# Two product groups to a PSUM bank, longer leads, and an accumulator that one engine touches: a graph network on one Trainium2 core

## The chip, the core and the metric

The kernel runs on one core of one Trainium2 chip. A core has five engines with a queue of instructions each: TensorE (PE in the profile, with its weight loads as PEld), VectorE (DVE), ScalarE (ACT), GpSimd (POOL) and SyncE (SP). PSUM, where TensorE writes its products, has eight banks of 512 float32 columns in 128 partitions. The metric is the device time of one execution in microseconds; lower is better. Three runs of the kernel before took 34,501.49, 34,504.76 and 34,556.67 us.

## The reference

There are 30,000 nodes with 128 features and 960,000 edges that are sorted by destination. Two layers are computed: a relational convolution, applied twice, and a gated one. Cut to what matters:

```python
def rel(h, basis, coeff, bias):              # basis [8,128,128], coeff [32,8]
    W = einsum('rb,bdf->rdf', coeff, basis)  # one matrix for each of 32 edge types
    msg = einsum('nd,rdf->nrf', h, W)[src, etype32] * weight
    return segment_sum(msg, dst) + bias

h = relu(layernorm(x))
x = x + rel(relu(rel(h, basis1, coeff1, bias1)), basis2, coeff2, bias2)

h = relu(layernorm(x))
for t in range(4):                           # one set of matrices for each of 4 edge types
    k, q, v = h @ Wk[t] + bk[t], h @ Wq[t] + bq[t], h @ Wv[t] + bv[t]
    msg = where(etype4 == t, sigmoid(k[dst] + q[src]) * v[src], 0)
    outs[t] = segment_sum(msg, dst) + h @ Ws[t] + b[t]
x = x + mean(outs)
```

## The kernel before

Edges are taken in tiles of 128, three tiles to a **group** (384 edges) and five groups to a **block**. Because edges are sorted, the destinations of a group lie within a window of 32 nodes. A preparation computes each edge's place in its window (`reld`) and index columns. Then come three **passes** over all edges: `c1` and `c2` (the two relational convolutions, `rel_body`) and `g` (the gated one, `gate_body`). Each pass is a loop of 25 iterations of 20 blocks, so 500 blocks, 2,500 groups and 7,500 tiles in all. An iteration is cut into four stages of five blocks.

The rows of the edges' sources are fetched from HBM by POOL, one indirect DMA for each tile (`gather`, L114), into a group's buffer `hg` (passes one and two) or `qv` (pass three, 1 KB a row); there are ten such buffers. The running sums of all nodes stand in SBUF as `agg` (128 features x 31,440 nodes). `add_windows` (L361) adds a block's five windows of 32 columns to it, at offsets that registers hold.

*Passes one and two.* With a group's rows come the edges' eight basis coefficients: `types` (L380) loads a block's edge types, `onehot` (L387, L392) makes a one-hot on VectorE and multiplies it with `coeff` on TensorE into `pc`, and `coefficients` (L401) scales them to `ce`. For each tile VectorE builds `sb` (L441), which holds the coefficient where the window column equals the edge's place, else zero, and TensorE multiplies it with the tile's rows into `pa` (L447; 8 x 32 columns, three tiles added up). ScalarE copies `pa` into the block's `ab` (L451). Once a block, `bases_out` (L409) multiplies `ab` with the eight basis matrices into `po`.

*Pass three.* For each group SP loads the window's keys `kw` (L485). `onehot` (L488, L494) compares the block's codes `kb` with `ic` and places with `iw`; `keys` (L501) multiplies one-hot and `kw` on TensorE into `pk`; VectorE adds the gathered queries (L542); ScalarE takes the sigmoid (L543). `sums` (L510, L512) multiplies by the values on VectorE and adds up by window on TensorE into `po`.

The order of all this is written out by hand (`tc.manual_schedule`); each engine runs its instructions in that order, and the framework adds the semaphore waits. The constants `iw` and `ic` stand in a PSUM tile `cp`, which also holds `pc`. `pa` has three banks, `po` two, `pk` four.

Beside the groups, `steps` finishes nodes whose sums are complete, 120 at a time: `after_first` writes the hidden layer and restarts the sums, `after_second` makes layer norm and the tables of keys, queries and values, `after_third` writes the result. Each such chain is spread over the following groups by the numbers in its list, and a new one starts every `PERIOD` (9) groups.

Of the kernel before, what the change touches and what calls it, by code (L numbers as in the profile page):

```python
# [9 lines left out]
F32 = mybir.dt.float32  # L10
# [36 lines left out]
PERIOD = NG * VB // NPI - 1  # L47
# [22 lines left out]
def kernel(  # L70
# [177 lines left out]
    def node_weights(nodew):  # L248

        wall = nodew.tile([P, 3, T, D], F32, name="wall")  # L250
        ball = nodew.tile([P, 3, T, D], F32, name="ball")
        for a, (w, b) in enumerate(((wk, bk), (wq, bq), (wv, bv))):
            nc.sync.dma_start(wall[:, a], w.rearrange("t d f -> d t f"))
            nc.scalar.dma_start(ball[:, a].rearrange("p t f -> p (t f)"), rows_of(b, P))
        nc.vector.tensor_add(ball[:, 0], ball[:, 0], ball[:, 1])
        for w in (wall, ball):
            nc.vector.tensor_scalar(w[:, 2], w[:, 2], 1.0 / T, None, op0=ALU.mult)
        four = nodew.tile([P, T, D], F32, name="four")
        nc.sync.dma_start(four, ws.rearrange("t d f -> d t f"))
        wsm = nodew.tile([P, D], F32, name="wsm")  # L260
        nc.vector.tensor_reduce(wsm, four.rearrange("p t f -> p f t"), AX.X, ALU.add)
        nc.vector.tensor_scalar(wsm, wsm, 1.0 / T, None, op0=ALU.mult)
        return wall, ball, wsm

    def node_tables(pool, ps, wall, ball, hn, krows, qvrows):
# [8 lines left out]
        for a in range(3):  # L274
            pw = ps.tile([P, T, D], F32, name="pw", bufs=4)
            nc.tensor.matmul(pw.rearrange("p t f -> p (t f)"), lhsT=hT,
                             rhs=wall[:, a].rearrange("p t f -> p (t f)"), start=True, stop=True)
            if a == 1:
                nc.scalar.copy(to[a], pw)
            else:  # L280
                nc.vector.tensor_add(to[a], pw, ball[:, a])
# [8 lines left out]
    def sorted_path():  # L290
        with ExitStack() as all_:
# [8 lines left out]
            def edge_pass(name, body, after, banks):  # L300


                with ExitStack() as held:
                    weights = held.enter_context(tc.tile_pool(name=f"{name}_w", bufs=1))
                    steps, run = after(weights), body(weights)
                    with tc.tile_pool(name=f"{name}_io", bufs=NQ) as io, \
# [8 lines left out]
                        nc.vector.tensor_copy(ic, icol)  # L315
                        with tc.For_i(0, NI, 1, iteration_sync="staggered") as i:
                            with tc.manual_schedule():
# [5 lines left out]
                                assert W < TQ * 4 * B and max(todo) < NG  # L323
# [5 lines left out]
                                run(i, io, pool, ps, cp, iw, ic, beside)  # L329
# [33 lines left out]
            def rel_body(table, weights, cof):  # L363
                def start(npool):
                    bas = npool.tile([P, B, D], F32, name="bas")
                    nc.scalar.dma_start(bas, weights.rearrange("b d f -> d b f"))
                    return lambda *args: body(bas, *args)

                def body(bas, i, io, pool, ps, cp, iw, ic, beside):
# [8 lines left out]
                    def types(s):  # L378
                        er[s] = pool.tile([P, TQ, TP], I32, name="er")
# [5 lines left out]
                    def onehot(s):  # L385
                        oh[s] = pool.tile([P, TQ, TP], F32, name="oh")
                        nc.vector.tensor_scalar(oh[s], er[s], icol4, None, op0=ALU.is_equal)  # L387
                        at = (1 + s % 2) * TQ * 4 * B
                        pc[s] = cp[:TP, at:at + TQ * 4 * B].rearrange("p (c q b) -> p c q b",
                                                                      c=TQ, q=4)  # L390
# [15 lines left out]
                    def bases_out(s):  # L406
                        po[s] = ps.tile([P, S, W], F32, name="po")
# [7 lines left out]
                    types(0)  # L415
                    onehot(0)
                    coefficients(0)
                    types(1)
                    onehot(1)
                    for s in range(NS):  # L420
# [9 lines left out]
                        if s + 2 < NS:  # L430
                            types(s + 2)
                        ab[s] = pool.tile([P, B, S, W], F32, name="ab")
                        for g in range(S):
# [4 lines left out]
                            pa = ps.tile([P, B, W], F32, name="pa", bufs=3)  # L438
                            for j in range(G):
                                sb = pool.tile([TP, B, W], F32, name="sb", bufs=12)  # L440
# [15 lines left out]
                            if g == 3 and s + 2 < NS:  # L456
                                onehot(s + 2)
                            if g == 3 and s > 1:
                                add_windows(po[s - 2], base[(s - 2) // SB], s - 2)
# [4 lines left out]
                    for s in (NS - 2, NS - 1):  # L464
# [3 lines left out]
            def gate_body(i, io, pool, ps, cp, iw, ic, beside):  # L468
# [7 lines left out]
                def types(s):  # L476
                    kb[s] = pool.tile([P, S, GE + GAP], F32, name="kb")[:, :, :GE]
# [20 lines left out]
                def keys(n):  # L498
                    pk[n] = ps.tile([TP, G, D], F32, name="pk", bufs=4)
# [5 lines left out]
                def sums(n):  # L505
                    s, g = n // S, n % S
                    if g == 0:
                        po[s] = ps.tile([P, S, W], F32, name="po")
# [9 lines left out]
                for n in range(S):  # L518
                    window(n)
                onehot(0)  # L520
                keys(0)
                for n in range(NG):
# [8 lines left out]
                    if g == 0 and s + 1 < NS:  # L531
                        types(s + 1)
# [7 lines left out]
                    if n + 1 < NG:  # L540
                        keys(n + 1)
# [4 lines left out]
                    if g == 1 and s + 1 < NS:  # L546
                        onehot(s + 1)
                    if g == 4 and s:
                        add_windows(po[s - 1], base[(s - 1) // SB], s - 1)
# [5 lines left out]
                add_windows(po[NS - 1], base[NQ - 1], NS - 1)  # L555


            def after_first(weights):

                def steps(at, pool, ps):  # L560
                    xt = pool.tile([VB, D], F32, name="xt", bufs=2)
                    r = pool.tile([P, VB], F32, name="r")
                    h = pool.tile([VB, D], F32, name="h")
                    cols, rows = agg[:, ds(at, VB)], ds(at, VB)
# [5 lines left out]
                    def relu():  # L570
                        nc.scalar.activation(r, cols, AF.Relu, bias=b1c)
# [7 lines left out]
                    def copy():  # L579
                        nc.scalar.copy(h, got["pr"])  # L580
                        nc.vector.tensor_scalar(cols, got["px"], b2c, None, op0=ALU.add)
# [4 lines left out]
                    return (0, load), (1, relu), (3, turn), (4, copy), (5, store)  # L586
                return steps

            def after_second(weights):
# [9 lines left out]
                def steps(at, pool, ps):  # L599
                    cols, rows = agg[:, ds(at, VB)], ds(at, VB)  # L600
                    xs = pool.tile([P, VB], F32, name="xs", bufs=2)
# [4 lines left out]
                    hT = pool.tile([P, VB], F32, name="hT")  # L606
                    kt = pool.tile([VB, T, D + GAP], F32, name="kt")[:, :, :D]
                    qvt = pool.tile([VB, T, 2 * D + GAP], F32, name="qvt")[:, :, :2 * D]
                    got = {}
# [5 lines left out]
                    def copy():  # L615
                        nc.scalar.copy(xs, cols)

                    def rows_():
                        nc.tensor.transpose(bank("px", VB, D), xs, ident)

                    def stats():
                        nc.vector.bn_stats(st, got["px"])
                        nc.vector.bn_aggr(mv, st)
                        nc.scalar.activation(rs, mv[:, 1:2], AF.Sqrt, bias=eps[:VB])

                    def norm_():
                        nc.vector.reciprocal(rs, rs)
                        nc.vector.tensor_scalar(hn, got["px"], mv[:, 0:1], rs, op0=ALU.subtract,
                                                op1=ALU.mult)

                    def turn():
                        nc.tensor.transpose(bank("pt", P, VB), hn, ident[:VB, :VB])

                    def relu():
                        nc.scalar.activation(hT, got["pt"], AF.Relu)

                    def weight(a):
                        def go():
                            nc.tensor.matmul(bank(a, VB, T * D), lhsT=hT,  # L639
                                             rhs=wall[:, a].rearrange("p t f -> p (t f)"),  # L640
                                             start=True, stop=True)
                        return go

                    def biased(a, to):
                        def go():
                            pw = got[a].rearrange("p (t f) -> p t f", t=T)
                            if a == 1:
# [285 lines left out]
```

## Time and profile before

| | |
|---|---|
| median of three runs | 34,504.76 us |
| the profiled execution's own time | 34,720.42 us |
| its span | 34,718.6 us |
| mean granted TensorE clock | 0.673 of full speed |
| busy: TensorE / weight loads / VectorE / ScalarE / POOL | 20,388 / 17,659 / 12,654 / 3,605 / 21,314 us |
| gathers for `hg` (L114) | 15,000, 14,224 us busy, 948 ns each |
| gathers for `qv` (L114) | 7,500, 7,088 us busy, 945 ns each |
| `sb` on VectorE (L441) | 15,000, 475 ns each |
| product matmuls (L447) | 30,000 instructions, 466 ns each |
| copies of products on ScalarE (L451) | 5,000, 373 ns each |

All durations come from this one profiled execution, whose own time is 216 us above the median of the runs. Lines of a timeline give start and duration in us, engine, line, operation, output and inputs, how many were merged, and in brackets how long the engine had been idle and what released it. A line of the list of waits gives who waited for whom: total us, times, longest. A "TensorE" matmul in float32 appears as two instructions.

### The profile page before, as it was taken

The page shows a single profiled execution, that of the slowest core. Times are in us where ns is not written, and L with a number is a line of the kernel's source. Part 1 is how long each engine was busy: PE and PEld are TensorE (multiplying, and loading weights), DVE is VectorE, ACT ScalarE, POOL GpSimd, SP SyncE. Part 2 cuts the span into 40 slices and gives each one's busy share as a digit, 9 for nine tenths or more (in the row PEclk, how much of TensorE's full clock was granted, in tenths as well). Part 3 has the DMA queues.
Part 4 walks back from the last instruction along what each step waited for, and adds up shares of the span by engine and source line. Part 5 has one row for each costly group of instructions (what it writes and reads, how often), then busy time and mean ns, then how long its engine had stood idle before and what let it go on. Part 6 is the DMA issues. An engine that isn't in the chain of part 4 may idle for free. (4 is left out here: it accounts for less than half of the span.)

```text
span 34718.6 us, 320544 instructions
## 1 busy us (share of the span) xinstructions
PE 20388.3 (59%) x87408; PEld 17658.9 (51%) x87408; DVE 12654.0 (36%) x33403; ACT 3604.7 (10%) x9717; POOL 21313.7 (61%) x22513
## 2 busy tenths in 40 slices
PE   3555555555555566666666666665555555555555
PEld 2444444444444445545445555545555555555555
DVE  4333333333333333333333333333333333333333
ACT  1000000000000011111111111111111111111111
POOL 3666666666666566666666666656666666666665
PEclk8777777777777777777777777765555555555555
DMA  3222222222222222222222222234444444444444
GB/s 111 60 60 60 59 61 60 60 59 60 59 60 59 68 73 73 73 73 73 73 73 72 73 73 73 73 103 144 143 144 144 145 144 145 144 144 143 143 143 140
DMA packets 2168060, 3244.36 MB, mean 93 GB/s; under 512 B 550283, under 2 KB 1540859, under 8 KB 2166350
## 3 DMA queue, kind: packets, MB, share of 16 engines
q0 software_dynamic: 840000, 1967.52, 21.2%
q1 hardware_dynamic: 982940, 997.80, 8.8%
q10 hardware_dynamic: 343410, 258.04, 2.6%
q8 instruction: 853, 13.98, 0.2%
q14 instruction: 857, 7.02, 0.1%
HBM read 2969.29 MB, written 252.28 MB: 93 GB/s over the span
## 5 line engine op out<-in xcount | busy, mean ns | idle before, releaser
L114 POOL DMA_INDIRECT hg<-h,idx x15000 | 14224.3, 948 | 8721.2 <-issue 4498.6
L447 PE MATMUL pa<-sb,hg 128*128 128x256 f32 x30000 | 9229.5, 466 | 5599.4 <-issue 2652.1
L447 PEld LDWEIGHTS pa<-sb,hg 128*128 128x128 f32 x30000 | 6930.6, 240 | 7333.1 <-issue 2969.4
L114 POOL DMA_INDIRECT qv<-qvtab,qi x7500 | 7087.9, 945 | 4645.7 <-issue 2252.6
L441 DVE SCALAR_TENSOR_TENSOR sb<-cp,relc,ce 128x256 f32<-128x256 f32 x15000 | 6124.2, 475 | 6625.4 <-remote 4458.6
L512 PE MATMUL po<-sel,msg 128*128 128x32 f32 x15000 | 3460.4, 387 | 4649.2 <-DVE msg L510 3763.7
L512 PEld LDWEIGHTS po<-sel,msg 128*128 128x128 f32 x15000 | 3424.0, 328 | 4936.1 <-DVE msg L510 3937.4
L501 PE MATMUL pk<-kw,kb 128*128 128x128 f32 x15000 | 3969.9, 438 | 241.1 <-DVE kb L488 183.3
L542 DVE TENSOR_TENSOR pk<-pk,qv 128x384 f32<-128x384 f32 x2500 | 1404.8, 562 | 7008.3 <-remote 4711.3
L451 ACT COPY ab<-pa 128x256 f32<-128x256 f32 x5000 | 1818.4, 373 | 20240.9 <-remote 9335.6
L501 PEld LDWEIGHTS pk<-kw,kb 128*128 128x128 f32 x15000 | 3464.0, 331 | 243.8 <-issue 243.8
L409 PE MATMUL po<-ab,bas 128*128 128x160 f32 x16000 | 2425.9, 306 | 456.7 <-ACT ab L451 243.9
L409 PEld LDWEIGHTS po<-ab,bas 128*128 128x128 f32 x16000 | 2356.3, 196 | 542.9 <-ACT ab L451 264.9
L361 DVE TENSOR_TENSOR agg<-agg,po 128x32 f32 x7500 | 1398.1, 186 | 2853.5 <-remote 789.9
L392 PE MATMUL cp<-coeff,oh 128*128 128x32 f32 x8000 | 1314.0, 294 | 1786.3 <-issue 1299.6
L392 PEld LDWEIGHTS cp<-coeff,oh 128*128 128x128 f32 x8000 | 1387.6, 235 | 1813.7 <-issue 1610.4
L543 ACT ACTIVATE pk<-pk 128x384 f32<-128x384 f32 x2500 | 1185.3, 475 | 9401.4 <-DVE pk L542 5999.8
L639 PE MATMUL bank<-wall,hT 128*120 128x512 f32 x1572 | 1011.8, 764 | 729.5 <-issue 286.6
L510 DVE TENSOR_TENSOR msg<-pk,qv 128x384 f32<-128x384 f32 x2500 | 1364.5, 546 | 137.7 <-remote 130.1
L488 DVE TENSOR_TENSOR kb<-kb,cp 128x1920 f32<-128x1920 f32 x500 | 1071.5, 2143 | 50.2 <-issue 30.4
L639 PEld LDWEIGHTS bank<-wall,hT 128*120 128x120 f32 x1572 | 347.2, 235 | 1008.1 <-issue 543.2
L650 DVE TENSOR_TENSOR kt<-bank,ball 120x512 f32<-120x512 f32 x262 | 181.1, 691 | 1457.7 <-remote 497.6
(77 smaller groups left out, 3740.7 us busy)
## 6 DMA issues: line engine op xcount, KB each, us to landing
kb<-kcode SPq DMA_DIRECT2D x500, 960.0 KB
er<-in_et_row SPq DMA_DIRECT2D x1000, 256.0 KB
hg<-h,idx POOLq DMA_INDIRECT x15000
kw<-ktab SPq DMA_DIRECT2D x2500, 64.0 KB
qvtab<-qvt ACTq DMA_DIRECT2D x262, 480.0 KB
qv<-qvtab,qi POOLq DMA_INDIRECT x7500
ktab<-kt ACTq DMA_DIRECT2D x262, 240.0 KB
xt<-in_x SPq DMA_DIRECT2D x262, 60.0 KB
```

The source lines that it names most:

```text
L114: nc.gpsimd.indirect_dma_start(out=to, out_offset=None, in_=table, in_offset=bass.IndirectOffsetOnAxis(ap=idx, axis=0))
L361: nc.vector.tensor_add(to, to, po[:, g, :])
L392: nc.tensor.matmul(pc[s][:, c].rearrange("p q b -> p (q b)"), lhsT=oh[s][:, c, :], rhs=cof.rearrange("p q b -> p (q b)"), start=True, stop ...
L409: nc.tensor.matmul(po[s].rearrange("p s w -> p (s w)"), lhsT=bas[:, b, :], rhs=ab[s][:, b].rearrange("p s w -> p (s w)"), start=(b == 0), ...
L441: nc.vector.scalar_tensor_tensor(sb, iw[:TP].unsqueeze(1).to_broadcast([TP, B, W]), relc[:, t0 + j:t0 + j + 1], ce[s].rearrange("p q c b - ...
L447: nc.tensor.matmul(pa.rearrange("p b w -> p (b w)"), lhsT=hg[:, j, :], rhs=sb.rearrange("p b w -> p (b w)"), start=(j == 0), stop=(j == G ...
L451: nc.scalar.copy(ab[s][:, :, g, :], pa)
L501: nc.tensor.matmul(pk[n][:, j, :], lhsT=kb[n // S][:, n % S, j * TP:(j + 1) * TP], rhs=kw[n], start=True, stop=True)
L510: nc.vector.tensor_mul(msg, pk[n], qv[n][:, :, 1, :])
L512: nc.tensor.matmul(po[s][:, g, :], lhsT=msg[:, j, :], rhs=sel[s][:, g * G + j, :], start=(j == 0), stop=(j == G - 1))
L542: nc.vector.tensor_add(pk[n], pk[n], qv[n][:, :, 0, :])
L639: nc.tensor.matmul(bank(a, VB, T * D), lhsT=hT, rhs=wall[:, a].rearrange("p t f -> p (t f)"), start=True, stop=True)
```

## The change

- **Product groups.** `pa` was a tile with three buffers of one bank each. It becomes eight halves of four fixed one-bank tiles, `pa0` to `pa3`; group number n of an iteration takes half n mod 8.
- **Sums.** In passes one and two `po` was a tile with two banks; it becomes three thirds of one bank, `pb`. In pass three `po` becomes two parts of the tile `cp`, and the two banks go to `pk`, which has six instead of four.
- **Leads.** In passes one and two edge types and one-hot run three blocks ahead instead of two (`er` and `oh` with three buffers, `sb` with sixteen instead of twelve), and the windows of a block are added three blocks later instead of two. In pass three keys are multiplied three groups ahead instead of one, `kb` has three buffers, the one-hot moves from a block's group 1 to group 0, and the windows of a block are added at group 0 two blocks later instead of at group 4 one block later.
- **Node steps.** `agg` is read and written by VectorE alone; copies on either side bring the values to and from the other engines. The chain of `after_second` is spread over 28 groups instead of 11, with its products leaving PSUM by ScalarE and its biases added by VectorE in SBUF. `PERIOD` is 8. The loading of the weights uses a temporary pool.

The diff, cut to its core:

```diff
-PERIOD = NG * VB // NPI - 1
+PERIOD = 8
...
                 def start(npool):
                     bas = npool.tile([P, B, D], F32, name="bas")
...
+                    def fixed(cp, cps):
+                        n = TQ * 4 * B
+                        pc = [cp[:TP, q * n:(q + 1) * n].rearrange("p (c q b) -> p c q b",
+                                                                   c=TQ, q=4) for q in (1, 2)]
+                        n = B * W
+                        pa = [cps.tile([P, 2 * n], F32, name=f"pa{q}") for q in range(4)]
+                        pa = [t[:, q * n:(q + 1) * n].rearrange("p (b w) -> p b w", b=B)
+                              for t in pa for q in range(2)]
+                        n = S * W
+                        pb = cps.tile([P, 4 * D], F32, name="pb")
+                        po = [pb[:, q * n:(q + 1) * n].rearrange("p (s w) -> p s w", s=S)
+                              for q in range(3)]
+                        return lambda *args: body(bas, pc, pa, po, *args)
+                    return fixed
...
-                        er[s] = pool.tile([P, TQ, TP], I32, name="er")
+                        er[s] = pool.tile([P, TQ, TP], I32, name="er", bufs=3)
...
-                        oh[s] = pool.tile([P, TQ, TP], F32, name="oh")
+                        oh[s] = pool.tile([P, TQ, TP], F32, name="oh", bufs=3)
...
-                        po[s] = ps.tile([P, S, W], F32, name="po")
+                        po[s] = pos[s % 3]
...
-                            pa = ps.tile([P, B, W], F32, name="pa", bufs=3)
+                            pa = pas[(s * S + g) % 8]
                             for j in range(G):
-                                sb = pool.tile([TP, B, W], F32, name="sb", bufs=12)
+                                sb = pool.tile([TP, B, W], F32, name="sb", bufs=16)
...
-                            if g == 3 and s + 2 < NS:
-                                onehot(s + 2)
-                            if g == 3 and s > 1:
-                                add_windows(po[s - 2], base[(s - 2) // SB], s - 2)
+                            if g == 3 and s + 3 < NS:
+                                onehot(s + 3)
+                            if g == 3 and s > 2:
+                                add_windows(po[s - 3], base[(s - 3) // SB], s - 3)
...
+            def gate_start(cp, cps):
+                n = S * W
+                po = [cp[:, 2 * W + q * n:2 * W + (q + 1) * n].rearrange("p (s w) -> p s w", s=S)
+                      for q in range(2)]
+                return lambda *args: gate_body(po, *args)
...
-                    kb[s] = pool.tile([P, S, GE + GAP], F32, name="kb")[:, :, :GE]
+                    kb[s] = pool.tile([P, S, GE + GAP], F32, name="kb", bufs=3)[:, :, :GE]
...
-                    pk[n] = ps.tile([TP, G, D], F32, name="pk", bufs=4)
+                    pk[n] = ps.tile([TP, G, D], F32, name="pk", bufs=6)
...
-                        po[s] = ps.tile([P, S, W], F32, name="po")
+                        po[s] = pos[s % 2]
...
-                    if n + 1 < NG:
-                        keys(n + 1)
+                    if n + 3 < NG:
+                        keys(n + 3)
                     nc.vector.tensor_add(pk[n], pk[n], qv[n][:, :, 0, :])
                     nc.scalar.activation(pk[n], pk[n], AF.Sigmoid)
                     if n > 1:
                         sums(n - 2)
-                    if g == 1 and s + 1 < NS:
+                    if g == 0 and s + 1 < NS:
                         onehot(s + 1)
-                    if g == 4 and s:
-                        add_windows(po[s - 1], base[(s - 1) // SB], s - 1)
+                    if g == 0 and s > 1:
+                        add_windows(po[s - 2], base[(s - 2) // SB], s - 2)
...
     # after_first
-                        nc.scalar.activation(r, cols, AF.Relu, bias=b1c)
+                        nc.vector.tensor_scalar(r, cols, b1c, 0.0, op0=ALU.add, op1=ALU.max)
...
-                        nc.vector.tensor_scalar(cols, got["px"], b2c, None, op0=ALU.add)
+                        nc.scalar.activation(fresh, got["px"], AF.Identity, bias=b2c)
...
+                    def restart():
+                        nc.vector.tensor_copy(cols, fresh)
...
-                    return (0, load), (1, relu), (3, turn), (4, copy), (5, store)
+                    return (0, load), (1, relu), (3, turn), (4, copy), (5, store), (9, restart)
...
     # after_second
-                    return ((1, copy), (2, rows_), (3, stats), (4, norm_), (5, turn), (6, relu),
-                            (7, weight(0)), (7, weight(1)),
-                            (8, biased(0, kt)), (8, biased(1, qvt[:, :, :D])),
-                            (8, weight(2)), (8, part),
-                            (9, biased(2, qvt[:, :, D:])), (9, own), (9, store(knode, kt)),
-                            (10, store(qvnode, qvt)))
+                    return (
+                        (0, lambda: nc.vector.tensor_copy(xs, cols)),
+                        (1, lambda: nc.tensor.transpose(bank("px", VB, D), xs, ident)),
+                        (2, lambda: nc.scalar.copy(xr, got["px"])),
+                        (6, stats),
+                        (7, lambda: nc.scalar.activation(rs, mv[:, 1:2], AF.Sqrt, bias=eps[:VB])),
+                        (11, norm_),
+                        (12, lambda: nc.tensor.transpose(bank("pt", P, VB), hn,
+                                                         ident[:VB, :VB])),
+                        (13, lambda: nc.scalar.activation(hT, got["pt"], AF.Relu)),
+                        (18, lambda: weight(0)),
+                        (19, lambda: nc.scalar.copy(kt, types(0))),
+                        (21, lambda: weight(1)),
+                        (22, lambda: nc.scalar.copy(qvt[:, :, :D], types(1))),
+                        (22, lambda: weight(2)),
+                        (23, lambda: nc.vector.tensor_add(kt, kt, ball[:VB, 0])),
+                        (23, lambda: nc.scalar.copy(vt, types(2))),
+                        (24, lambda: store(knode, kt)),
+                        (24, lambda: nc.tensor.matmul(bank("po", P, VB), lhsT=wsm, rhs=hT,
+                                                      start=True, stop=True)),
+                        (25, lambda: nc.scalar.activation(part, got["po"], AF.Identity, bias=bsc)),
+                        (26, lambda: nc.vector.tensor_add(vt, vt, ball[:VB, 1])),
+                        (27, lambda: store(qvnode, qvt)),
+                        (27, lambda: nc.vector.tensor_add(cols, xs, part)))
...
     # after_third
-                        nc.scalar.copy(c, agg[:, ds(at, VB)])
+                        nc.vector.tensor_copy(c, agg[:, ds(at, VB)])
```

## The prediction, made before the changed kernel was run

> **What bounds the kernel now.** I first cut the span at the first and last gather of each pass (busy time by window: every engine, then TensorE's clock, DMA share, GB/s).
>
> ```profile
> 335.00:11576.00 11241.00, 6348.05 (x27428) 5469.35 (x27429) 3800.81 (x11223) 1010.60 (x2992) 7127.53 (x7500) 0.73 0.23 60
> 11630.00:22948.00 11318.00, 7191.12 (x29420) 5680.44 (x29421) 4378.82 (x12715) 1179.33 (x3490) 7096.52 (x7500) 0.78 0.27 73
> 23080.00:34682.00 11602.00, 6720.55 (x30168) 6431.34 (x30168) 4199.89 (x8471) 1326.13 (x3019) 7087.92 (x7500) 0.51 0.47 144
> ```
>
> Each pass issues 7500 gathers from POOL. One is busy 0.95 us and in an undisturbed stream the next starts 0.30 us later, so a block of 15 gathers needs 18.75 us. The passes take 22.5, 22.6 and 23.2 us a block (11,241, 11,318 and 11,602 over 500). POOL thus stands still 3.7, 3.9 and 4.45 us a block, 6.0 ms in all: no change of waits can win more. Then the list of all waits:
>
> ```profile
> ACT ab L451 <- remote: 9335.6, 1058, 70.1
> ...
> POOL hg L114 <- issue: 4498.6, 12552, 332.7
> DVE sb L441 <- remote: 4458.6, 491, 32.9
> ...
> POOL hg L114 <- remote: 2025.0, 828, 5.7
> POOL qv L114 <- DVE msg L510: 1752.4, 448, 15.6
> ...
> DVE sb L441 <- PE cp L392: 1631.9, 335, 18.2
> ```
>
> "Remote" is a semaphore update that matches no recorded end of work, and it holds ScalarE for 9.3 ms. The timeline of one block of pass one shows whose it is:
>
> ```profile
> 6007.55 1.46 PE L447 MATMUL pa<-sb,hg 128*128 128x256 f32 x6
> 6009.06 1.47 PE L447 MATMUL pa<-sb,hg 128*128 128x256 f32 x6
> 6010.36 0.97 PE L392 MATMUL cp<-coeff,oh 128*128 128x32 f32 x8
> 6016.74 0.94 POOL L114 DMA_INDIRECT hg<-h,idx  x1 [0.30 <-issue]
> 6020.76 0.65 ACT L451 COPY ab<-pa 128x256 f32<-128x256 f32 x2 [14.81 <-remote]
> 6020.82 0.34 DVE L581 TENSOR_SCALAR agg<-bank,b2c 128x120 f32 x1 [14.39 <-remote]
> 6020.99 0.95 POOL L114 DMA_INDIRECT hg<-h,idx  x1 [3.31 <-remote]
> 6021.12 4.79 DVE L441 SCALAR_TENSOR_TENSOR sb<-cp,relc,ce 128x256 f32<-128x256 f32 x12
> ```
>
> TensorE's products of groups 2 and 3 are recorded as done at 6009.0 and 6010.5, yet ScalarE's two copies, VectorE and POOL all wait until 6020.8. TensorE's completions become visible ten microseconds late, and then together, about 3 us after POOL's stream of gathers stopped (at 6017.7) for want of a free `hg`. One block later it repeats. The cycle is: POOL uses up its ten buffers and stops, the late completions arrive, buffers come free, POOL restarts. Why completions lag while gathers stream the profile doesn't tell; that each block holds about one such stop it does (idle POOL over 1 us: 604, 741 and 607 times in the passes of 500 blocks). Pass three:
>
> ```profile
> 28019.03 1.63 PE L501 MATMUL pk<-kw,kb 128*128 128x128 f32 x6
> 28024.51 0.95 POOL L114 DMA_INDIRECT qv<-qvtab,qi  x1 [0.31 <-issue]
> 28028.15 0.57 DVE L542 TENSOR_TENSOR pk<-pk,qv 128x384 f32<-128x384 f32 x1 [9.49 <-remote]
> 28028.63 0.55 DVE L510 TENSOR_TENSOR msg<-pk,qv 128x384 f32<-128x384 f32 x1
> 28029.44 0.95 POOL L114 DMA_INDIRECT qv<-qvtab,qi  x1 [3.99 <-DVE msg L510]
> 28030.02 2.14 DVE L488 TENSOR_TENSOR kb<-kb,cp 128x1920 f32<-128x1920 f32 x1
> ```
>
> Here VectorE's add waits for late keys until 2.7 us after POOL stopped at 28025.5; add and `msg` then free a `qv` within 1.3 us. The one-hot (L488) comes after that release, in the shadow of the running gathers.
>
> **The change part by part.** *Sums in `cp` (pass three).* `po` moves into the tile from which L488 and L494 read `ic` and `iw`. That columns of one tile don't overlap doesn't help: L441 reads only `iw` and L392 writes only `pc`, both in `cp`, yet the last wait above stands between them, and no `sb` of group 4 in the 900 blocks that have one starts before that L392 ends. So the one-hot and add_windows, now at group 0 right behind sums(n-2), wait for the sums just issued, the newest work in TensorE's queue. Behind the one-hot on VectorE are the five adds into `agg`, the next add and the next `msg`, which frees the `qv` that POOL wants. When this wait falls into the late state, the chain from the completions to POOL grows by L488 2.14 + L494 0.65 + five adds 5 x 0.19, 3.7 us, less what add and `msg` overlap. New stop: 2.7 + 3.7 + 1.1 + 0.2 = 7.7 us, less the ordinary 0.30: 7.4 against 4.45 a block, +2.95 us, 500 times: **+1.5 ms**. Least: 0 if the wait ends while POOL has buffers; most +1.85 ms (3.7 x 500).
>
> *Keys three groups ahead, six `pk`, three `kb`.* The add's wait (4.7 ms on remote, 1.6 ms on L501) disappears there, but the one-hot inherits it: keys(n+3) stands ahead of sums(n-2) on TensorE. Gain 0 as long as that wait is once a block; if it weren't, at most 4.45 - 3.2, 0.6 ms. On SP's queue the loads keep their places: `kw` for group n+5 is issued at group n, so keys(n+3) have two groups of lead (7.5 us) instead of four, and the third `kb` lets the 960 KB load of codes go a block earlier. TensorE waited 20 us for `kw` in the whole pass; I take 0, and if `kw` came late it would add to the same stop.
>
> *Two product groups in a bank.* By the same evidence L447 of every odd group waits for ScalarE's copy of the even one, 0.37 us plus two hand-overs; behind it on TensorE queue bases_out and the next coefficients. 2500 pairs x 0.37 = 0.9 ms of TensorE's time, which its 56 to 64% busy share hides while completions are prompt. In the late state it stops TensorE from running ahead, so fewer products are finished when POOL stops. From none to one more stop of 3.0 us in every second block (1000 blocks: +1.5 ms).
>
> The Trainium skill speaks against this part: "Perfetto Trace Analysis", Optimizing Tensor Performance, asks independent groups to rotate through different PSUM banks so that one's evacuation overlaps the next one's matmuls. By that rule all 0.9 ms would be paid. The copy row sits in before beside other products, three banks apart, so no run here shows that yet.
>
> *`po` in `pb`, coefficients three blocks ahead.* add_windows at group 3 now waits for the bases_out of the same block's group 1; VectorE would wait at group 4 for L392 anyhow, so five adds (0.95 us) move behind the late completions. POOL is released there by TensorE, not by VectorE: 0 to 0.9 ms, taken 0.1. The third `er`, `oh` and 16 `sb` buy nothing, because the group 4 wait on `cp` stays.
>
> *Node steps spread out, `agg` left to VectorE.* This removes L581's wait (1128 us remote in pass one), the waits of the adds on ScalarE (562 us on `xs`) and of L650 on fresh products. What can be won is the stops beyond one a block: 104 x 3.0 + 241 x 2.5 = 0.9 ms. I take 0.6, since the L392 wait remains. The added copies (0.3 to 0.7 us, 262 times) lie on ScalarE, busy 10%, and VectorE, 36%. Weight loading changes once, nothing.
>
> I take +0.9 for the pairs, between its ends because pass two, with its chain of node matmuls, already has 137 stops more than pass one and loses only 0.1 ms by them. Sum: 34.72 + 1.5 + 0.9 + 0.1 - 0.6 = 36.6 ms for a profiled execution (34,720 now). The median of the runs is 0.6% below it, 34,505: **36,400 us**.
>
> **The rivals.** *Faster.* If the one-hot's wait ends while POOL still has buffers, since keys are issued three groups earlier and VectorE runs ahead, passes one and two win 0.9 and pass three 0.6: 33,000. Deciding point: the completions that sums(n-2) needs must come within 18 us without a stop. For it: long waits on keys exist today. Against: completions came only after a stop in the blocks shown.
>
> *Much slower.* Pairs cost a second stop in every block of passes one and two: 1000 x 3.0 = 3.0 ms, with pass three 39,000. For it: TensorE is blocked at every second group. Against: pass two above.
>
> *No effect.* Stops are set by POOL's ten buffers alone, which stay: 34,500.
>
> **How the numbers follow.** Forecast 0.58, faster 0.23, much slower 0.15, no effect 0.04. About 0.2% (70 us) can be told from no change: faster 0.23, same 0.04, slower 0.73. The range takes in most of the slower case and the weaker half of the faster: 33,400 to 38,300.
>
> **What would show it.** Right: L488 waits several microseconds, on TensorE, once a block; POOL's stop in pass three grows from 4 to about 7.5 us and 26 us pass per block; L447 waits for L451 at every second group; passes one and two stay between 22 and 24 us a block. Wrong: L488 waits for nothing, or POOL's stream runs over several blocks unbroken.

## The result and the profile after

The changed kernel took 36,048.86 us (median of four runs, 36,015.11 to 36,143.56) beside 34,503.94 us of the kernel before: ratio 1.0444, 95% interval 1.0431 to 1.0458, slower. Its profiled execution took 36,143.56 us with a span of 36,141.7 us, 1,423 us more than that of before. Lines moved a little in the source: the one-hot is now L513 and L519, the add into `pk` L569, `msg` L535, `sums`' matmuls L537, `add_windows` L367, the products L466, their copies L470 and the coefficients' matmuls L410.

The three passes, cut at their first and last gather (busy time by window, in the columns of the first view above):

```profile
342.00:11595.00 11253.00, 6577.05 (x27426) 5402.82 (x27426) 3848.65 (x11457) 1017.73 (x2992) 7112.07 (x7500) 0.76 0.21 60
11658.00:23000.00 11342.00, 7253.20 (x29420) 5735.13 (x29420) 4343.16 (x12954) 1486.91 (x4239) 7183.16 (x7500) 0.79 0.26 73
23137.00:36101.00 12964.00, 6508.93 (x30171) 6342.00 (x30172) 4244.62 (x8724) 1268.00 (x2771) 7089.91 (x7500) 0.51 0.42 129
```

Passes one and two grew by 12 and 24 us, pass three by 1,362 us, from 23.2 to 25.9 us a block. The whole loss is in pass three. The list of all waits shows who is new in it:

```profile
DVE kb L513 <- remote: 7167.0, 449, 17.2
...
DVE agg L367 <- remote: 5968.3, 561, 19.1
PEld pa L466 <- ACT ab L470: 5398.6, 1081, 13.5
...
POOL qv L114 <- DVE msg L535: 2884.3, 400, 8.2
```

The one-hot waits 449 times in 500 blocks, 16 us each, for a late completion (before it waited 50 us in all), and POOL's wait for `msg` grew from 1,752 to 2,884 us. "Remote" names no engine, but the semaphore whose update ended the wait does: in all 449 cases it is one that TensorE's instructions alone update, and the last of these with a recorded end lies 8.4 us (median) before the update. One stop in the timeline:

```profile
28017.68 0.95 POOL L114 DMA_INDIRECT qv<-qvtab,qi  x1 [0.30 <-issue]
28021.56 2.15 DVE L513 TENSOR_TENSOR kb<-kb,cp 128x1920 f32<-128x1920 f32 x1 [16.87 <-remote]
...
28023.63 0.65 DVE L519 TENSOR_TENSOR sel<-cp,relc 128x480 f32<-128x480 f32 x1
28024.19 1.07 DVE L367 TENSOR_TENSOR agg<-agg,cp 128x32 f32 x5
28025.18 0.57 DVE L569 TENSOR_TENSOR pk<-pk,qv 128x384 f32<-128x384 f32 x1
28025.66 0.55 DVE L535 TENSOR_TENSOR msg<-pk,qv 128x384 f32<-128x384 f32 x1
...
28026.47 0.94 POOL L114 DMA_INDIRECT qv<-qvtab,qi  x1 [7.85 <-DVE msg L535]
```

POOL's last gather ends at 28018.6. VectorE's next instruction starts 2.9 us later, when the completions arrive, as before; but it is now the one-hot, not the add. One-hot, `sel` and five adds into `agg` run before the add and the `msg` that frees a `qv`. POOL stands still for 7.85 us where it stood for 4.

### The profile page after: what moved, and what is told of

Its sections match the earlier page's. It is cut to its first block, busy times and chain, and to the rows that moved or that the text cites. A ratio compares the mean times of both kernels' runs of the same rounds, so it can differ in the third digit from the quotient of the medians.

```text
span 36141.7 us, 322232 instructions
## 1 busy us (share of the span) xinstructions
PE 20462.3 (57%) x87408; PEld 17555.0 (49%) x87408; DVE 12720.0 (35%) x34189; ACT 3875.9 (11%) x10241; POOL 21386.7 (59%) x22513
## 5 line engine op out<-in xcount | busy, mean ns | idle before, releaser
L466 PE MATMUL pa<-sb,hg 128*128 128x256 f32 x30000 | 9632.8, 475 | 7978.4 <-ACT ab L470 4886.4
L466 PEld LDWEIGHTS pa<-sb,hg 128*128 128x128 f32 x30000 | 6843.4, 239 | 10348.5 <-ACT ab L470 5398.6
L537 PE MATMUL cp<-sel,msg 128*128 128x32 f32 x15000 | 3358.2, 381 | 6140.0 <-DVE msg L535 6018.6
L537 PEld LDWEIGHTS cp<-sel,msg 128*128 128x128 f32 x15000 | 3418.4, 328 | 6312.2 <-DVE msg L535 6183.2
L470 ACT COPY ab<-pa 128x256 f32<-128x256 f32 x5000 | 1842.3, 372 | 19997.7 <-remote 9015.8
L367 DVE TENSOR_TENSOR agg<-agg,pb 128x32 f32 x5000 | 942.1, 188 | 8072.3 <-remote 5479.7
L513 DVE TENSOR_TENSOR kb<-kb,cp 128x1920 f32<-128x1920 f32 x500 | 1076.8, 2154 | 7216.6 <-remote 7167.0
L427 PEld LDWEIGHTS pb<-ab,bas 128*128 128x128 f32 x16000 | 2403.5, 199 | 122.9 <-ACT ab L470 29.8
L427 PE MATMUL pb<-ab,bas 128*128 128x160 f32 x16000 | 2450.1, 308 | 23.1 <-ACT ab L470 12.0
L410 PEld LDWEIGHTS cp<-coeff,oh 128*128 128x128 f32 x8000 | 1427.2, 253 | 869.3 <-issue 729.2
L410 PE MATMUL cp<-coeff,oh 128*128 128x32 f32 x8000 | 1334.7, 318 | 771.7 <-DVE oh L407 640.4
L569 DVE TENSOR_TENSOR pk<-pk,qv 128x384 f32<-128x384 f32 x2500 | 1408.7, 563 | 640.1 <-PE pk L526 314.0
L535 DVE TENSOR_TENSOR msg<-pk,qv 128x384 f32<-128x384 f32 x2500 | 1371.6, 549 | 270.5 <-PE cp L537 191.1
L367 DVE TENSOR_TENSOR agg<-agg,cp 128x32 f32 x2500 | 466.5, 187 | 610.1 <-remote 488.7
L407 DVE TENSOR_SCALAR oh<-er,icol 128x512 f32<-128x512 int32 x1000 | 478.1, 482 | 118.9 <-issue 81.3
```

The lines of the kernel that those rows point to most:

```text
L367: nc.vector.tensor_add(to, to, po[:, g, :])
L410: nc.tensor.matmul(pc[s][:, c].rearrange("p q b -> p (q b)"), lhsT=oh[s][:, c, :], rhs=cof.rearrange("p q b -> p (q b)"), start=True, stop ...
L427: nc.tensor.matmul(po[s].rearrange("p s w -> p (s w)"), lhsT=bas[:, b, :], rhs=ab[s][:, b].rearrange("p s w -> p (s w)"), start=(b == 0), ...
L466: nc.tensor.matmul(pa.rearrange("p b w -> p (b w)"), lhsT=hg[:, j, :], rhs=sb.rearrange("p b w -> p (b w)"), start=(j == 0), stop=(j == G ...
L470: nc.scalar.copy(ab[s][:, :, g, :], pa)
L535: nc.vector.tensor_mul(msg, pk[n], qv[n][:, :, 1, :])
```

## The experiments

I measured the stops of pass three in each trace in one way: the time from the end of POOL's last gather to the next one where it exceeds 1 us, the first VectorE instruction after it, and what VectorE runs until POOL goes on. For each kernel this is the commonest kind of stop:

| kernel | such stops, of all | median stop, us | first VectorE work after | VectorE runs until POOL restarts |
|---|---|---|---|---|
| before | 348 of 607 | 4.23 | 2.93 | add, `msg` |
| after | 300 of 517 | 7.81 | 2.89 | one-hot, `sel`, five adds, add, `msg` |
| e6 own bank | 291 of 559 | 5.53 | 3.23 | five adds, add, `msg` |
| e7 `cp` only | 281 of 633 | 5.14 | 2.80 | five adds, add, `msg` |
| e10 order only | 310 of 708 | 4.22 | 2.93 | add, `msg` |

**Gate pass alone, passes one and two alone, pairs apart, own bank (e1 to e4).** The edits:

```diff
# e1_gate_only: before, with gate_start and gate_body of after (and its copy in after_third)
# e2_rel_only:  after, with gate_body of before
# e3_apart: after, and
-                              for t in pa for q in range(2)]
+                              for q in range(2) for t in pa]
# e4_own_bank: after, and
-                po = [cp[:, 2 * W + q * n:2 * W + (q + 1) * n]...
+                pb = cps.tile([P, 4 * D], F32, name="pb")
+                po = [pb[:, q * n:(q + 1) * n]...
...
-                    pk[n] = ps.tile([TP, G, D], F32, name="pk", bufs=6)
+                    pk[n] = ps.tile([TP, G, D], F32, name="pk", bufs=5)
...                                                        # and keys(n + 2), not n + 3
```

> Before, with the gate pass of after alone (sums in cp, keys three groups ahead, one-hot and add_windows at group 0); the product groups, bases_out and node steps are those of before. Theory (the one-hot waits in every block for the sums just issued into its bank): the whole loss of 1.54 ms less the 0.04 of passes one and two, about 35,900 to 36,000 us, pass three at 25.9 us per block. Rival (the banks shared by two product groups pay part of the loss): under 35,500 us.

> After, with the gate pass of before: product groups two to a bank, coefficients three blocks ahead, po in pb and the spread node steps stay. Theory (only the gate pass loses): 34,500 to 34,600 us, all three passes within 0.2 us per block of before. Rival of the prediction's sum (pairs +0.9, po +0.1, node steps -0.6): 34,900 us.

> After, with the eight product groups so laid out that consecutive groups lie in different banks (a bank comes back after four groups, not after one). If sharing a bank costs what the prediction took (+0.9 ms, hidden by node steps that win 0.6): 35,150 us. If it costs nothing because the copy of 0.37 us lies beside other work and POOL's stop sets the block: 36,050 us, within 0.2%, though the products' wait for the copy disappears.

> After, with the sums of pass three in a bank of their own (both halves in it), one key buffer and one group of lead less. Theory (the shared tile makes the one-hot wait): the one-hot waits for keys or loads alone, add_windows at group 0 still waits for the new sums, so the stop keeps 2.7 + five adds 0.95 + 1.1 + 0.2 = 5 us less 0.3 = 4.7 per block against 4.45: about 34,700 us. Rival (the new order, one-hot and add_windows at group 0 ahead of the next add, costs by itself): 35,800 to 36,100 us.

All four expectations missed, because the kernel before itself took 28,875.16 us here, on another chip. The ratios were 0.9969 (0.9958 to 0.9981), 1.0022 (1.0013 to 1.0032), 0.9991 (0.9982 to 1.0001) and 1.0007 (0.9998 to 1.0017). Pass three of e1 in the view of busy time by window, then the wait and one occurrence of the shared-bank one-hot in e3 (list of waits; timeline):

```profile
19320.00:28732.00 9412.00, 6759.41 (x30232) 6374.06 (x30232) 4324.98 (x8736) 1268.62 (x2774) 7090.11 (x7500) 0.52 0.58 177
```

```profile
DVE kb L513 <- PE cp L537: 763.9, 450, 4.3
```

```profile
24018.32 2.15 DVE L513 TENSOR_TENSOR kb<-kb,cp 128x1920 f32<-128x1920 f32 x1 [1.58 <-PE cp L537]
```

The same wait is there, 450 times, but it lasts 1.7 us, ends with a recorded TensorE instruction and not with "remote", and POOL doesn't stop: 18.8 us a block, its bare stream. On this chip TensorE's completions are prompt and POOL bounds all three passes. The granted clock of pass three is 0.52 here and 0.51 in after, so the clock doesn't explain the difference there (in passes one and two it is 0.82 and 0.83 in e1, 0.73 and 0.78 in before). In this regime the gate pass of after even wins: 9,411 us between its first and last gather in e1 beside 9,504 us for that of before in e2.

**The changed kernel once more (e5).** No edit.

> The changed kernel itself, once more. In the four runs before this one no pass shows late completions of TensorE, POOL's stream runs unbroken for hundreds of microseconds, and before takes 28,875 us in place of 34,504. Theory (the loss of 1.54 ms is the one-hot's wait multiplied by late completions): where these lag, the ratio is 1.044; where they are prompt, the wait ends while POOL still has buffers and the ratio is 0.998 to 1.001, about 28,850 us beside 28,875. Rival (the shared tile costs VectorE, and so the time, in either case): 1.02 or more.

It ran on a chip where before takes 34,774.17 us: 36,486.80 us, ratio 1.05 (1.0483 to 1.0518). Its one-hot waits 448 times on remote, 7,302 us in all, and its passes take 11,321, 11,422 and 13,153 us. The first half of the theory is met; e1 and e3 carry the other half, since after itself wasn't run on the prompt chip. All runs that follow are from chips where completions lag (before at 34,757 to 34,783 us).

**Own bank, where completions lag (e6).** The kernel of e4.

> The kernel with the sums of pass three in a bank of their own, as before in this study, for a place where TensorE's completions lag (before at 34,500 to 34,800 us, after 1.05 times that). Theory (the shared tile makes the one-hot, 2.8 us with sel, wait for the newest sums): one-hot and sel leave the chain behind the late completions, add_windows stays in it: the stop is 2.7 + five adds 0.95 + 1.1 + 0.2 - 0.3 = 4.7 us per block in place of 7.2, ratio 1.00 to 1.01. Rival (the new order costs by itself, or the keys' wait takes its place): ratio 1.04 to 1.05. Where completions are prompt: 1.00, as measured.

35,483.90 us, ratio 1.0209 (1.0192 to 1.0226): between the two ranges, in neither. Pass three takes 12,162 us, 1,004 less than with the sums in `cp` on the same chip (e8 below). A stop in its timeline:

```profile
28033.02 0.86 DVE L367 TENSOR_TENSOR agg<-agg,pb 128x32 f32 x4 [12.34 <-remote]
28034.09 0.19 DVE L367 TENSOR_TENSOR agg<-agg,pb 128x32 f32 x1 [0.22 <-DVE agg L367]
28034.23 0.57 DVE L570 TENSOR_TENSOR pk<-pk,qv 128x384 f32<-128x384 f32 x1
28034.70 0.55 DVE L536 TENSOR_TENSOR msg<-pk,qv 128x384 f32<-128x384 f32 x1
...
28035.52 0.94 POOL L114 DMA_INDIRECT qv<-qvtab,qi  x1 [5.76 <-DVE msg L536]
```

One-hot and `sel` have left the chain, and the stop is shorter by 2.3 us. The wait didn't go: it moved to `add_windows`, which reads one half of a bank while the newest sums are written to the other half (e10 below gives each half its own).

**Shared bank alone (e7).**

```diff
# e7_cp_only: before, and
-                        po[s] = ps.tile([P, S, W], F32, name="po")
+                        at = 2 * W + s % 2 * S * W
+                        po[s] = cp[:, at:at + S * W].rearrange("p (s w) -> p s w", s=S)
```

> Before, with one edit: the sums of pass three lie in cp beside ic and iw instead of a bank of their own; keys, order and all else as before. Theory (the bank alone makes the one-hot wait for sums(n-2), which TensorE has just been given): where completions lag, one-hot 2.15 and sel 0.65 us come into the chain, with add_windows left at group 4: stop +1.9 to +2.8 us per block, +0.95 to +1.4 ms, ratio 1.03 to 1.04. Rival (it takes the new order or the keys' lead as well): under 1.01. Where completions are prompt: 1.00.

35,588.68 us, ratio 1.0237 (1.022 to 1.0254); pass three 12,439 us. One bank shared costs half of the loss (1.0489 in e8 on the same chip) with nothing else changed, somewhat less than expected and not through the instruction I named. The commonest stop, then a line of the list of waits:

```profile
28062.32 0.95 POOL L114 DMA_INDIRECT qv<-qvtab,qi  x1 [0.31 <-issue]
28066.16 1.09 DVE L361 TENSOR_TENSOR agg<-agg,cp 128x32 f32 x5 [10.09 <-remote]
28067.27 0.57 DVE L543 TENSOR_TENSOR pk<-pk,qv 128x384 f32<-128x384 f32 x1
28067.75 0.55 DVE L511 TENSOR_TENSOR msg<-pk,qv 128x384 f32<-128x384 f32 x1
...
28068.57 0.94 POOL L114 DMA_INDIRECT qv<-qvtab,qi  x1 [5.30 <-DVE msg L511]
```

```profile
DVE kb L488 <- PE cp L513: 1187.4, 392, 3.4
```

The first wait of VectorE that meets late completions is now `add_windows` at group 4, and its five adds (1.1 us) come into the chain. This commonest stop is the smaller part of the loss. POOL's stops over 1 us in pass three take 3,130 us, beside 2,368 in before, and 69 of them are longer than 9 us, 678 us together, beside 15 and 201 us. One of the 69:

```profile
23432.66 1.08 DVE L361 TENSOR_TENSOR agg<-agg,cp 128x32 f32 x5 [9.88 <-remote]
23438.18 0.57 DVE L543 TENSOR_TENSOR pk<-pk,qv 128x384 f32<-128x384 f32 x1 [4.43 <-issue]
...
23439.47 0.94 POOL L114 DMA_INDIRECT qv<-qvtab,qi  x1 [9.98 <-DVE msg L511]
```

Behind the adds VectorE's queue here also holds the loading of the next stage's window offsets into registers (`bases`, L348). It keeps VectorE's next add back by 4.2 to 4.8 us in 67 of the 69, so it too stands between the late completions and the `msg` that frees a `qv`.

The one-hot at group 1 also waits for the shared bank, 392 times, but 3.0 us each, right after the late completions have come, while gathers run again. So the bank makes the wait, and the place in the block sets its price.

**Pairs apart, where completions lag (e8).** The kernel of e3.

> The kernel with consecutive product groups in different banks, for a place where completions lag. If pairs in a bank cost what the prediction took (+0.9 ms, offset by 0.6 of the node steps): ratio to before 1.02 to 1.03. If POOL's stops hide the copy, the ratio of after stays: 1.044 to 1.05, and passes one and two keep 22.5 us per block.

36,470.92 us, ratio 1.0489 (1.0471 to 1.0506). Passes one and two take 11,363 and 11,383 us, 22,746 together; e6, with pairs as in after and on the same chip, 11,318 and 11,418, 22,735 (all rounded at the end). The wait did what it should:

```profile
PEld pa L466 <- ACT ab L470: 1290.9, 150, 14.9
```

In after there were 1,081 such waits, 5.4 ms; 150 are left, with 1.3 ms, and the time doesn't move.

**More buffers (e9).**

```diff
# e9_more_buffers: before, and
-                            hg = pool.tile([TP, G, D], F32, name="hg", bufs=10)
+                            hg = pool.tile([TP, G, D], F32, name="hg", bufs=14)
-                    qv[n] = pool.tile([TP, G, 2, D], F32, name="qv", bufs=10)
+                    qv[n] = pool.tile([TP, G, 2, D], F32, name="qv", bufs=14)
```

> Before, with 14 buffers for the gathers in place of 10 (hg and qv). Theory (POOL stops when its buffers are used up and late completions arrive only when it stops; a cycle is then 4 groups longer, 9 in place of 5): where completions lag, some 280 stops a pass in place of 500 to 600, 2.0 to 2.4 ms less, ratio 0.93 to 0.94. Rival (the lateness is set by the work given to TensorE or by a wait of VectorE once per block, so the stop comes once per block whatever the buffers): ratio 0.99 to 1.00. Where completions are prompt: 1.00.

35,944.92 us, ratio 1.0345 (1.0327 to 1.0362): a clear miss, and slower. The stops over 1 us hardly became fewer (608, 700 and 557, beside 604, 741 and 607 in before), and the commonest stop of pass three is as long as before (311 times 4.25 us). What grew are stops over 9 us: 530, 602 and 933 us in the three passes beside 201, 109 and 201. They stand at fixed places: 24 in each pass before the first gather of an iteration, and 24 more in pass three before the 49th; in before all 42 stand before an iteration's 31st gather, the first that uses one of the ten buffers (three gathers each) a second time. Apart from the 1st, 31st and 49th gathers POOL stands still 11,647 us in the three passes, beside 11,951 in before (the 0.3 us between gathers included): 0.3 ms less, where 2.0 to 2.4 were expected. So more buffers left the commonest stop, once a block, as it was; they lost the time at fixed places of an iteration, for a reason that no run shows.

**Order alone (e10).**

```diff
# e10_gate_order: after, and
-                po = [cp[:, 2 * W + q * n:2 * W + (q + 1) * n].rearrange(...)
+                po = [cps.tile([P, 4 * D], F32, name=f"po{q}")[:, :n].rearrange(...)
                       for q in range(2)]
...
-                    pk[n] = ps.tile([TP, G, D], F32, name="pk", bufs=6)
+                    pk[n] = ps.tile([TP, G, D], F32, name="pk", bufs=4)
...                                                        # and keys(n + 1), not n + 3
```

> After, with each half of the sums of pass three in a bank of its own (as in before), four key buffers and keys one group ahead (as in before); the new order (one-hot and add_windows at group 0, in that order) stays. Theory (only waits for the newest sums in a shared bank cost; with a bank for both halves add_windows still had one): no wait of the one-hot or add_windows on TensorE is left, pass three takes 23.2 to 23.4 us per block, ratio 1.00 to 1.005. Rival (the new order itself is the rest of the loss, since one bank for the sums gave back only some 1.0 of 1.56 ms): pass three stays at 24.3, ratio 1.015 to 1.02. Where completions are prompt: 1.00.

34,995.70 us, ratio 1.006 (1.0043 to 1.0077). Pass three takes 11,642 us, 23.28 a block and 1,511 us less than e5 on the same chip:

```profile
27942.03 0.95 POOL L114 DMA_INDIRECT qv<-qvtab,qi  x1 [0.30 <-issue]
27945.98 0.57 DVE L568 TENSOR_TENSOR pk<-pk,qv 128x384 f32<-128x384 f32 x1 [4.71 <-remote]
27946.46 0.55 DVE L535 TENSOR_TENSOR msg<-pk,qv 128x384 f32<-128x384 f32 x1
...
27947.27 0.95 POOL L114 DMA_INDIRECT qv<-qvtab,qi  x1 [4.29 <-DVE msg L535]
```

The add is the first instruction behind the completions again, and the stop has its old length. The list of waits has the add's wait of before back, and the one-hot no longer waits for TensorE at all:

```profile
DVE pk L568 <- remote: 4165.5, 665, 13.1
...
DVE kb L513 <- issue: 29.8, 24, 1.3
...
DVE kb L513 <- DMA kb<-kcode: 24.5, 2, 12.3
```

Pass three is some 110 us longer than the gate pass of before on the same chip (11,532 us in e11). That lies at the starts of iterations (POOL stands still 311 us before the 31st gathers, 170 us in e11), and not in the stop that comes once a block. e10 also takes back the keys' lead, from three groups to one, which no run changes by itself; e7, with order and lead of before, shows what the shared bank costs alone.

**What sets one stop per block (e11, e12).**

```diff
# e11_pc_apart: e2, and
+                        pc = cps.tile([P, 4 * D], F32, name="pc")          # no longer in cp
...
-                        pa = [cps.tile([P, 2 * n], F32, name=f"pa{q}") for q in range(4)]
+                        pa = [cps.tile([P, 2 * n], F32, name=f"pa{q}") for q in range(3)]
...
-                              for t in pa for q in range(2)]
+                              for q in range(2) for t in pa]
...
+                            if g == 0 and s > 1:                           # was g == 3, s - 3
+                                add_windows(po[s - 2], base[(s - 2) // SB], s - 2)
# e12_wide_bases: before, and
-                            if g == 1 and s:
-                                bases_out(s - 1)
+                            if g == 1 and s and s % 2 == 0:
+                                bases_out(s - 2)                           # 320 columns, two blocks
...
```

> Gate pass of before; passes one and two of after, with the coefficient sums pc in a bank apart from iw, three banks of product pairs laid out apart, and add_windows moved ahead of the next bases_out, so that every wait of VectorE on TensorE in the edge work has four groups (15 us) of lead. Theory V (VectorE's wait for the newest coefficients, once per block, sets one stop per block): the stops over 1 us of passes one and two fall from 600 to 750 to half or less, 0.9 ms less a pass, ratio 0.95. Theory C (TensorE's own backlog sets them: a stop each time some 110 to 130 of its instructions, a block's worth, have gone): both passes stay at 22.5 to 22.8 us per block, ratio 1.00. Where completions are prompt: 1.00.

> Before, with bases_out once for two blocks (twice as wide): 16 of TensorE's 110 to 118 recorded instructions per block go in passes one and two, add_windows comes a block later. Theory C (a stop for every block's worth of TensorE instructions): 13 to 15 in 100 of the idle time of POOL go, 0.25 ms a pass, ratio 0.985. Theory V (one stop per wait of VectorE): 1.00, passes one and two at 22.5 to 22.7 us per block. Where completions are prompt: 1.00.

e11: 34,624.58 us, ratio 0.9955 (0.9938 to 0.9971), the only kernel here that beats both where completions lag; its passes one and two take 11,289 and 11,246 us, beside 11,317 and 11,453 in e10 with the layout of after. That is some 0.2 ms, not the 1.8 ms of theory V, and none of it comes from the stop that recurs in every block: POOL stands still 150 us less before the 31st gathers (600 beside 750), its gathers take 100 us less, and elsewhere nothing changes (7,701 us of standstill beside 7,686). The stops over 1 us are 579 and 643, far from half. The reason is in its waits:

```profile
DVE agg L367 <- remote: 3706.2, 320, 31.8
DVE agg L367 <- PE pa L467: 3312.1, 312, 17.6
```

Four groups of lead aren't enough: `add_windows` still waits in most blocks. So theory V in its strong form, that no wait of VectorE at all would mean no stop, wasn't put to the test. e12: 35,052.83 us, ratio 1.0079 (1.0062 to 1.0096). TensorE's recorded instructions in pass one fell by 15% (54,857 to 46,847), the stops over 1 us from 604 to 585 and from 741 to 674, but passes one and two grew to 11,484 and 11,470 us. Theory C as I sized it falls: fewer instructions didn't win time, also not apart from the starts of iterations (745 us before the 31st gathers beside 446 in before, 7,989 us of standstill elsewhere beside 7,888). e12 also moves `add_windows`, widens the copies' target and loads the node weights through a temporary pool, so that it isn't a pure test. What makes a stop come once per block stays open.

## Why the prediction was right, and where not

The forecast (36,400, slower at 0.73) held; 36,049 lies 1% under it. The main term was right in mechanism and size; that the total came so close is in part luck, since two other sizes were wrong with opposite signs (+0.9 and -0.6) and left only 0.3 ms between them. By its own terms:

- *Sums in `cp`: +1.5 ms predicted, 1.36 ms measured* in pass three of the profiled pair; 1.51 ms between e5 and e10. The working holds to the instruction: 7.7 us predicted for a stop, 7.81 measured, made of the instructions named; 25.9 us a block where 26 were named. That the wait arises from columns of one tile that don't overlap is shown by e10 and e7. The Trainium skill, "PSUM — Partial Sum Buffer", section "PSUM bank collisions raise a hardware error", asks for such a wait: PSUM is to be guarded by bank and quadrant (32 partitions), not by address. The 449 waits of L513 for matmuls that write other columns agree. In every run here what shares a bank also shares a tile, so that which of the two the wait goes by isn't shown.
- *Keys three groups ahead: 0 predicted.* Nothing speaks against it, though no run changes the lead alone. The add's wait on remote (4.7 ms) went and the one-hot has 7.2 ms in its place; with keys one ahead (e10) the add has 4.2 ms again.
- *Two product groups to a bank: +0.9 predicted, nothing measured.* This step failed; what was measured is the lower of its two ends, 0 and 1.5. The wait came (1,081 times in 2,500 pairs, 5.4 ms on L470), but that "fewer products are finished when POOL stops" cost nothing: e8 takes three quarters of that waiting away and wins nothing. My reading, which no run tests, is that POOL's stop ends with the late completions, whenever TensorE did the work. The rule from the Trainium skill's "Perfetto Trace Analysis" that I weighed there asks for this overlap; here, with TensorE 58 and 64% busy in these passes, none of its price was paid.
- *Node steps and `agg` on VectorE: -0.6; `po` in `pb`: +0.1.* Together with the pairs these passes moved by +36 us, where the sum said +0.4 ms. Pairs cost nothing (e8), so they hide no gain: 0.6 ms net didn't come. The step that failed is that stops beyond one a block would go with the node steps' waits; there were 604 and 741 stops over 1 us in before and 708 and 721 in after. The +36 us are themselves a difference of two larger changes. Before the 31st gather of an iteration POOL stands still 706 us in after, 446 in before; everywhere else in the two passes it stands still 295 us less (7,593 beside 7,888). e6 and e7, which have the two layouts on one chip, say the same: 729 beside 447, and 7,703 beside 7,933. So a part of the gain came in the ordinary stops, which became shorter though not fewer, and the starts of iterations took it back. Which part of the change did either isn't shown. `add_windows` in `pb` has many late waits now (L367, 5.5 ms on remote in these passes, beside 0.65 for L361 in before). The node steps by themselves weren't run, nor `po` in `pb`.

The rivals: *Faster* rested on the one-hot's wait ending while POOL has buffers. That is what happens where completions are prompt (1.7 us, e3; 0.9969, e1), at a gain of 0.3% and not 4%, because there is hardly a stop to win. *Much slower* needed a price for pairs that e8 rules out. *No effect* said that POOL's buffers alone set the stops: e10 has ten as well, and after is 1.5 ms slower by what stands in the chain behind the completions.

## What to carry to other kernels

Once a wait meets a completion that comes late, its price is the work queued behind it on the same engine up to the instruction that frees the bound engine's buffer: count those instructions in the trace, and put the freeing ones first. Free columns of a PSUM tile aren't free if another engine reads that tile's bank: using them joins two chains that had nothing to do with each other, here at 0.8 ms (e7) to 1.4 ms (after) of 34.5. Where a profile shows many waits, ask which of them stand between the bound engine's stop and its restart; the others, like the pairs' 5 ms, may go or stay.

## What was unexpected of the hardware

The same program took 28.9 ms on one chip and 34.5 to 34.8 ms on others, at the same granted clock in pass three of the new order (0.52 in e1, 0.51 in after). The difference is the lateness of TensorE's completions beside POOL's stream of gathers: on the slower chips they arrive 2.8 to 3.2 us after the stream has stopped, on the other POOL streams unbroken at 18.8 us a block. VectorE's don't lag there: in the stop of after shown above `msg` ends at 28026.21 and POOL starts 0.26 us later. What causes it no run here shows. Nor is the chip parted from the occasion: e1 to e4 were measured on one chip on one occasion.
